# Keys' and values' block products move to a third PSUM bank, queries take turns with the other two, and the last sequence's output shares are cut by heads

## The chip, the cores and the metric

The kernel runs on one core of a Trainium2 chip. The metric is device time in microseconds (us) of one execution, lower is better. The core's engines are TensorE (PE; its weight loads are the row PEld), VectorE (DVE), ScalarE (ACT), GpSimd (POOL) and SyncE (SP, which issues the DMAs). They work side by side and wait for each other by semaphores.

## What is computed

The input is 16 sequences of 256 tokens with 256 features, float32. Two residual layers follow each other:

```python
x = x + attention(layernorm(x), wq, wk, wv, wo)
x = x + quantised_linear(layernorm(x), weight, bias)
```

The attention has 16 query heads and 4 key and value heads of 128 features each, four query heads to a group. A query sees the first 4 keys (the sink) and the last 32, its own among them. The linear layer rounds its input, row by row, and its weight, output row by output row, to whole numbers from -128 to 127, multiplies, scales back and adds the bias.

## The kernel before

**Units and slots.** A unit is (n, g, t): a sequence n (0 to 15), a group g (0 to 3) of four heads, and a half t of the 256 tokens. There are 128 units, in the order of the list `units` (line 693), in which two of the last sequence change places, so that it ends (15,2,0), (15,3,0), (15,2,1), (15,3,1). The main loop (line 769) goes through slots i = 0 to 129. In slot i TensorE computes the scores of unit i, turns the exponentials of unit i-1, and multiplies those by the values. Everything else is put into slots by hand: `chunks` (keys or values), `asked` (queries), `shares` (output projection), `early` and `small` (all the rest). `in_written_order` (line 21) then holds every engine to the order in which its instructions were written, so that an instruction that waits holds up all behind it on its engine.

**One slot.** `scores_and_turned` (line 475) interleaves four score products into the bank `pss` with four transposes into the bank `ptd`. ScalarE copies `ptd` to `ad`; VectorE scales and masks the scores (L497) and takes the maximum (L499); ScalarE takes four exponentials (L506); VectorE divides by the sums (L513 to L516, the function `normalised`). The next slot's transposes `ptd` need that result. `times_values` (line 518) writes `po`, in the pool `ps_m`, and ScalarE copies it to `oT` (L531).

**Products by seven.** From the second sequence on, queries, keys and values of a pair of heads are 256x256 products made of seven 128x128 block products instead of eight (`products`, line 251), from sums that GpSimd has made beforehand. A float32 product of 128x128 blocks is two matmul instructions, so a group has 14. `REGION` (line 225) gives each product its place: 2, 6, 1 and 7 fill the first bank of a pair, 4, 5 and 3 three quarters of the second. `combine` (line 264) then adds them up in five steps, L276 to L280: L276 and L277 read the first bank, L278 to L280 the second. For queries VectorE does it in the following slot, straight from PSUM (ScalarE first copies product 1, L291). For keys and values (a *chunk*) ScalarE copies both banks in the same slot, the small one first (`both_banks`, L297), and GpSimd combines from the copies.

A query group issues 1, 2, 6, 7 and then 4, 5, 3; a chunk issues 4, 5, 3 first (`SMALL_FIRST`). Query groups come in every slot; chunks in four slots out of eight: for sequence n in slots 8n-5 and 8n+1 (values), 8n-3 and 8n-1 (keys). Queries of the first sequence, and heads 14 and 15 of the last one, are plain products (L464).

**PSUM.** There are eight banks: one for `pss`, one for `ptd`, two for the output projection (`y0`, `y1`), two for queries, keys and values (`q0`, `q1`, pool `ps_q`), and two that take turns in the pool `ps_m`. The latter hold `po`, the transposed input `xt` (line 341, slot 8n-7 for sequence n), `ht` and `pa` of the linear layer (lines 620 and 627), and plain products. `ps_m` hands its two tiles out in turn: a request gets the one asked for the longer time ago, and its first matmul waits until that has been read.

**Output and linear layer.** `projected_fast` (line 561) projects a group's heads with the same seven products for sequences 1 to 14; `projected` (line 547) does plain products, four heads at a time, for the first and last sequence, in slot i+2 (i+3 for some). The linear layer is five steps, `ffn_steps` (line 590): stats, norm, quantise, turn, linear, one in each of five slots. The last sequence has a shorter form for each half of its tokens, `last_steps` (line 641), run in slots 127 to 128 for the first half and after the loop for the second.

Of the kernel before, what the change touches and what calls it, by code (L numbers as in the profile page):

```python
# [34 lines left out]
def kernel(  # L35
# [148 lines left out]
    def ffn_weight_steps():  # L184
        ws = p1.tile([P, NC], FP, name="ws")
        wq16 = p1.tile([P, NC, DM], BF, name="wq16")
        diag = p1.tile([P, NC, P], FP, name="diag")

        wr = p1.tile([P, NC], FP, name="wr")

        def scales():
            dve.tensor_reduce(ws, wf_sb, AX.X, ALU.max, apply_absolute_value=True)
            dve.tensor_scalar(ws, ws, 1e-8, 1.0 / 127.0, ALU.max, ALU.mult)
            dve.reciprocal(wr, ws)

# [12 lines left out]
        def turn():  # L208
            for c in range(NC):
                pt = ps_m.tile([P, NC, P], BF, tag="m", name=f"wt_{c}")  # L210
                for o in range(NC):
                    pe.transpose(pt[:, o, :], wq16[:, o, c * P : (c + 1) * P], ident16)
                act.copy(wqfT[:, c, :], pt.rearrange("p o n -> p (o n)"))
            pw = ps_m.tile([P, DM], FP, tag="m", name="pw")
            for c in range(NC):
                pe.matmul(pw[:, c * P : (c + 1) * P], ones, diag[:, c, :], start=True, stop=True)
            act.copy(wsc_bc, pw)

        return [scales, quantise, diagonals, narrow, turn]

# [1 line left out]

    REGION = {2: (0, 0), 6: (0, 1), 1: (0, 2), 7: (0, 3), 4: (1, 0), 5: (1, 1), 3: (1, 2)}

    def banks(pool_, tag, name):
        return [pool_.tile([P, NBLK, P], FP, tag=f"{tag}{k}", name=f"{name}_{k}") for k in range(2)]

    def region(p, i):  # L230
        return p[REGION[i][0]][:, REGION[i][1]]
# [27 lines left out]
            yield region(p, i), *pairs[i]  # L259


    SMALL_FIRST = (4, 5, 3, 1, 2, 6, 7)

    def combine(eng, p, p1, c11_u, v, c12, c21_c22):

# [156 lines left out]

    def keys(n, pair):

        p = banks(ps_q, "q", f"pk_{n}_{pair}")[::-1]
        for to, left, right in products(p, factors(n, wk_sb, wk_sums, pair), SMALL_FIRST):
            pe.matmul(to, left, right, start=True, stop=True)  # L427
        k = p1.tile([P, 2, 3, D], FP, tag="ktmp", name=f"ktmp_{n}_{pair}")
        kb = k[:, :, 0:2].rearrange("p e j (k i) -> p e (j k) i", i=QB)
        rest = lambda: keys_to(n, 2 * pair, kb)  # L430
        keys_late[rest] = 1 + pair
        return Products(p, f"k_{n}_{pair}", (k[:, 0, 0:3:2], k[:, 1, 2], k[:, 0, 1], k[:, 1, 0:2])), rest

    def values(n, pair):
        p = banks(ps_q, "q", f"pv_{n}_{pair}")[::-1]
        for to, left, right in products(p, factors(n, wv_sb, wv_sums, pair), SMALL_FIRST):
            pe.matmul(to, right, left, start=True, stop=True)  # L437
        v = p2.tile([P, 3, 2, D], FP, tag="vt", name=f"vt_{n}_{pair}")
        w = vw[n, pair] = p3.tile([NK, SB, 2 * D], FP, tag="vw", name=f"vw_{n}_{pair}")
        return Products(p, f"v_{n}_{pair}", (v[:, 0:3:2, 0], v[:, 2, 1], v[:, 1, 0], v[:, 0:2, 1])), (  # L440
            lambda: values_to(w, v.rearrange("p j e d -> p j (e d)"), range(NT))
        )

    def queries(n, h):

        g, hh = divmod(h, HG)
        if hh == 0:
            qt[n, g] = p2.tile([P, NT + 1, NBLK, HG, QB], FP, tag="qt", name=f"qt_{n}_{g}")
        q = qt[n, g]
        if fast_queries(n, h):  # L450
            p = banks(ps_q, "q", f"pq_{n}_{h}")
            for to, left, right in products(p, factors(n, wq_sb, wq_sums[:, g], h // 2)):
                pe.matmul(to, left, right, start=True, stop=True)  # L453
            return Products(
                p, f"q_{n}_{h}", (q[:, 0:3:2, :, hh], q[:, 2, :, hh + 1], q[:, 1, :, hh], q[:, 0:2, :, hh + 1])
            )
        if hh == 0:
            pq = ps_q.tile([P, NBLK, P], FP, tag="q0", name=f"pq_{n}_{h}")
            pq = pq.rearrange("p (e j) i -> p e (j i)", e=2)
        else:  # L460
            pq = ps_m.tile([P, 2, T], FP, tag="m", name=f"pq_{n}_{h}")
        for e in range(2):
            for c in range(NC):
                pe.matmul(  # L464
                    pq[:, e], wq_sb[:, c, (h + e) * D : (h + e + 1) * D], xnT[n][:, c, :],
                    start=(c == 0), stop=(c == NC - 1),
                )
        to = q[:, 0:NT, :, hh : hh + 2, :].rearrange("p t k h i -> p h (t k) i")
        return lambda: act.copy(to, pq.rearrange("p h (k i) -> p h k i", i=QB))
# [74 lines left out]
        t = [wo_sums[:, i, 2 * g : 2 * g + 2] for i in range(4)]  # L544
        right_sums(t, *(wo_half(g, p, half) for p in range(2) for half in range(2)))

    def projected(n, g, t):

        if (g, t) == (0, 0):
            pys[n] = banks(ps_y, "y", f"py_{n}")  # L550
        py, o = pys[n][t][:, 0:2].rearrange("p i d -> p (i d)"), oTs[n, g]
        last = n == B - 1
        if last and g == 0:
            pe.matmul(py, ident, xts[n][:, t, :], start=True, stop=False)
        for hh in range(HG):
            h = g * HG + hh
            pe.matmul(py, o[:, t, hh, :], wo_sb[:, h, :], start=(h == 0 and not last), stop=(h == H - 1))  # L557
        if g == G - 1 and not last:
# [2 lines left out]
    def projected_fast(n, g, part):  # L561

        if (g, part) == (0, 0):
            pys[n] = banks(ps_y, "y", f"py_{n}")
# [12 lines left out]
        if (g, part) == (G - 1, 1):  # L577
# [3 lines left out]
            def rest():  # L581
                sums.first()
                sums.combine(dve)
                xt = xts[n].rearrange("p t (i d) -> p (t i) d", d=D)
                (pool if n < B - 2 else dve).tensor_add(xt, xt, f[:, 0:4])

            return rest

# [52 lines left out]
    def last_steps(j):  # L641
# [2 lines left out]

        n, tag = B - 1, f"last_{j}"
        py = pys[n][j][:, 0:2].rearrange("p i d -> p (i d)")
        d, x2 = (p1.tile([P, NT, DM], FP, tag=k, name=f"{k}_{tag}")[:, 0] for k in ("h", "yo"))
        y = p1.tile([P, NT, DM], FP, tag="xn", name=f"y_{tag}")[:, 0]
        mv = p2.tile([P, nc.vector.BN_AGGR_DIM], FP, tag="mv2", name=f"mv_{tag}")
        top, by, xs = (p2.tile([P, 1], FP, tag=k, name=f"{k}_{tag}") for k in ("top", "by", "xs1"))  # L650
# [13 lines left out]
        def quantise():  # L664
            dve.tensor_scalar(top, top, mv[:, 1:2], 127e-12, ALU.mult, ALU.max)
            dve.reciprocal(by, top)
            dve.tensor_scalar(by, by, mv[:, 1:2], 127.0, ALU.mult, ALU.mult)
            dve.tensor_scalar(d, d, by, MAGIC, ALU.mult, ALU.add)
            dve.tensor_scalar(d, d, MAGIC + 127.0, MAGIC - 128.0, ALU.min, ALU.max)
            pool.tensor_scalar(xs, top, 1.0 / 127.0, None, ALU.mult)  # L670

        def turn():
            pt = ps_m.tile([P, NC, P], FP, tag="m", name=f"ht_{tag}")
            for c in range(NC):
                pe.transpose(pt[:, c], d[:, c * P : (c + 1) * P], ident)
            dve.tensor_scalar(hT, pt, MAGIC, None, ALU.subtract)

        def linear():
            pa = ps_m.tile([P, DM], FP, tag="m", name=f"pa_{tag}")
# [14 lines left out]
    units[-3], units[-2] = units[-2], units[-3]  # L694
    PER = G * NT

    chunks, early, asked, shares, small = {}, {}, {}, {}, {}

    def at(slot, f, what=small):
        what.setdefault(slot, []).append(f)  # L700

    for n in range(B):
        q = (-3, -2, -1, 0, 1, 2, 3, 4) if n < B - 1 else (-3, -2, -1, 0, 1, 2, 3, 3)
        if n == 0:
            q = (-1, -1, 0, 0, 1, 1, 2, 4)
            for slot, f in (
# [13 lines left out]
        at(max(first + 2, 2), lambda n=n: turned(n))  # L720
        at(max(first - 5, 0), lambda n=n: n > 1 and load_x(n))
    for i, (n, g, t) in enumerate(units):
        if not fast_output(n):
            late = n == 0 or i == (B - 1) * PER
            at(i + 3 if late else i + 2, lambda u=(n, g, t): projected(*u), shares)
        elif t == 1:
            for part in range(2):
                at(i + 2 + part, lambda u=(n, g, part): projected_fast(*u), shares)
# [3 lines left out]
        at((2, 3, 4, 6)[g], lambda g=g: weight_sums(wq_sb[:, :, g * HG * D : (g + 1) * HG * D], wq_sums[:, g]))  # L732
        at(7 + g, lambda g=g: output_weight_sums(g))
    at(0, other_loads)
    for slot, f in zip((3, 4, 7, 8, 10), ffn_weight_steps()):
        at(slot, f)
    steps = {}
    for n in range(B - 1):
        done = (n + 1) * PER + 2
        for k, slot in enumerate((1, 2, 3, 4, 5) if n < B - 2 else (0, 1, 2, 3, 4)):  # L740
            def step(n=n, k=k):
                if k == 0:
                    steps[n] = ffn_steps(n)
# [25 lines left out]
    for i in range(len(units) + 2):  # L769
# [3 lines left out]
        if waiting:  # L773
            waiting.first()
        shared = shares.pop(i, [])
        combined = [f() for f in shared]
        if u:
            sm = exponentials(*u, nmax)
        if waiting:
# [2 lines left out]
        rests = [f() for f in early.pop(i, []) if i]  # L782
        if not shared:
            rests += [queries(n, h) for n, h in asked.pop(i, []) if not fast_queries(n, h)]
        if i == len(units):
            tail[2]()
        values_out = times_values(*w) if w else None
        if chunk:
            chunk, chunk_rest = chunk()
            chunk.both_banks()  # L790
        if u:
            normalised(*u, sm)
        for f in rests:
            f()
        if w:
            values_out()
        for f in later.pop(i, []):
# [13 lines left out]
        for f in combined:  # L811
            if f:
                f()
        for f in small.pop(i, []):
            f()
        if i == len(units) - 1:
            tail = last_steps(0)
            for f in tail[:2]:
                f()
        if i == len(units):  # L820
            tail[3]()
    for f in last_steps(1):
        f()
    in_written_order(tc)
# [32 lines left out]
```

## Time and profile before

| what | value |
|---|---|
| median of 3 runs | 816.11 us (815.9 to 816.27) |
| the profiled execution | 816.0 us |
| its span, first to last instruction | 814.2 us |
| mean granted TensorE clock | 0.997 |
| instructions | 19607 |
| matmuls | 7082 |
| period of a sequence (eight slots) in the middle | about 49.3 us |
| HBM read and written | 9.83 MB and 4.19 MB |

In the profile, a row of a timeline gives the start in us, the busy time in us, the engine, the line, the operation, what is written and read, and the number of instructions; brackets tell for how long the engine had been idle and what ended that. The chain of waits goes back from the last instruction, at each step to what released it or to the instruction before it on its engine; its rows give start, length, engine, tile, line and count. L453 is line 453. The period above is the distance from the keys' first group at 393.10 us to that of the next sequence at 442.29 us, rounded.

### The profile page before, as it was taken

The numbers are of one execution on the slowest core, as the hardware profiler recorded it, in microseconds if no ns is written. First come the engines' busy times: TensorE is split into PE (matmuls) and PEld (weight loads), VectorE is DVE, ScalarE is ACT, GpSimd is POOL, SyncE is SP. The second block draws the span as 40 slices with busy tenths as digits, with TensorE's granted clock in tenths as the row PEclk, the third lists the DMA queues.
The fourth block names the chain that finished last, engine by engine and source line by source line (L and its number), as shares of the span: only waits on it lengthen the run. The fifth ranks groups of instructions, "written<-read, shape, count | busy, mean of one in ns | idle before, by whom it ended". The sixth has DMA issues, their size and how long they took to land.

```text
span 814.2 us, 19607 instructions
## 1 busy us (share of the span) xinstructions
PE 800.1 (98%) x7082; PEld 785.5 (96%) x7082; DVE 588.1 (72%) x1711; ACT 441.9 (54%) x1631; POOL 511.2 (63%) x809
## 2 busy tenths in 40 slices
PE   9999999999999999999999999999999999999995
PEld 7899999999999999999999999999999999999984
DVE  2567777787777877877777877877877777777665
ACT  3655555555556555555555555555555555555552
POOL 4667775676576675676666666665766766756422
PEclk9999999999999999999999999999999999999998
DMA  6510201011020110201102020110202102010100
GB/s 213 160 28 14 57 14 46 25 36 48 16 59 11 52 32 14 70 14 42 29 27 58 14 52 20 41 42 15 63 7 56 29 20 64 14 33 25 32 11 27
DMA packets 35633, 33.14 MB, mean 41 GB/s; under 512 B 5968, under 2 KB 34000, under 8 KB 35536
## 3 DMA queue, kind: packets, MB, share of 16 engines
q1 hardware_dynamic: 35536, 31.87, 14.2%
q8 instruction: 57, 0.93, 0.5%
q14 instruction: 40, 0.33, 0.1%
HBM read 9.83 MB, written 4.19 MB: 17 GB/s over the span
## 4 chain that ended last, share of the span: by engine, by line
PE 95%; DVE 2%; ACT 1%; issue 0%; DMA 0%; POOL 0%; DVEq 0%; ACTq 0%; POOLq 0%
PE pq L453 23%; PE py L573 22%; PE po L522 14%; PE pss L486 11%; PE ptd L491 7%; PE pk L427 6%; PE pv L437 6%; PE py L557 3%; PE pq L464 1%; PE xt L344 1%; PE pa L630 1%; ACT s L506 1%; PE pv L399 0%; PE ht L623 0%; DMA x<-in_x_dram 0%
## 5 line engine op out<-in xcount | busy, mean ns | idle before, releaser
L494 ACT COPY ad<-ptd 68x512 f32<-68x512 f32 x128 | 74.4, 581 | 214.7 <-PE ptd L491 214.7
L506 ACT ACTIVATE s<-s,nmax 128x68 f32<-128x68 f32 x512 | 173.6, 340 | 18.8 <-DVE nmax L499 12.4
L486 PE MATMUL pss<-kt,qt 128*128 128x68 f32 x1024 | 152.5, 251 | 0.0
L486 PEld LDWEIGHTS pss<-kt,qt 128*128 128x128 f32 x1024 | 147.5, 191 | 0.8 <-issue 0.5
L491 PE MATMUL ptd<-ident,s 128*68 128x128 f32 x512 | 139.1, 273 | 1.8 <-ACT oT L531 1.0
L522 PE MATMUL po<-ad,vw 68*128 68x128 f32 x1024 | 135.4, 275 | 0.0
L497 DVE SCALAR_TENSOR_TENSOR s<-pss,masks 128x272 f32<-128x272 f32 x128 | 56.3, 440 | 108.8 <-PE pss L486 106.4
L522 PEld LDWEIGHTS po<-ad,vw 68*128 68x128 f32 x1024 | 125.7, 192 | 1.0 <-ACT ad L494 0.3
L453 PE MATMUL pq<-xs,wq_sums 128*128 128x128 f32 x714 | 118.7, 275 | 0.0
L453 PEld LDWEIGHTS pq<-xs,wq_sums 128*128 128x128 f32 x714 | 98.8, 192 | 0.0
L506 ACT ACTIVATION_READ_ACCUMULATOR s<-s,nmax 128x1 f32 x512 | 95.6, 187 | 0.0
L531 ACT COPY oT<-po 128x512 f32<-128x512 f32 x128 | 75.3, 588 | 28.8 <-PE po L522 28.8
L491 PEld LDWEIGHTS ptd<-ident,s 128*68 128x68 f32 x512 | 84.5, 165 | 2.3 <-ACT oT L531 2.3
L573 PE MATMUL py<-wo_sums,os 128*128 128x128 f32 x672 | 84.2, 275 | 0.0
L276 POOL TENSOR_TENSOR ktmp<-b_k 128x256 f32<-128x256 f32 x30 | 21.9, 729 | 94.7 <-ACT b_k L297 94.7
L573 PEld LDWEIGHTS py<-wo_sums,os 128*128 128x128 f32 x672 | 79.4, 192 | 0.0
L240 POOL TENSOR_TENSOR os<-oT 128x256 f32<-128x256 f32 x56 | 46.2, 825 | 43.9 <-ACT oT L531 42.1
L276 POOL TENSOR_TENSOR vt<-b_v 128x256 f32<-128x256 f32 x30 | 21.8, 728 | 82.8 <-ACT b_v L297 82.8
L453 PE MATMUL pq<-xnT,wq_sb 128*128 128x128 f32 x476 | 72.7, 275 | 0.0
L453 PEld LDWEIGHTS pq<-xnT,wq_sb 128*128 128x128 f32 x476 | 62.7, 192 | 0.2 <-ACT b_v L297 0.2
L516 DVE TENSOR_TENSOR s<-s,sm 128x272 f32<-128x272 f32 x128 | 58.9, 460 | 4.4
L573 PE MATMUL py<-wo_sb,oT 128*128 128x128 f32 x448 | 59.2, 275 | 0.0
(182 smaller groups left out, 1845.4 us busy)
## 6 DMA issues: line engine op xcount, KB each, us to landing
vw<-vt SPq DMA_DIRECT2D x192, 64.0 KB, 2.0
vw<-vt SPq DMA_DIRECT2D x160, 32.0 KB, 2.4
x<-in_x_dram SPq DMA_DIRECT2D x16, 256.0 KB
out_dram<-y SPq DMA_DIRECT2D x15, 256.0 KB, 2.1
wq_sb<-in_wqT_dram SPq DMA_DIRECT2D x4, 512.0 KB, 9.4
wo_sb<-in_woT_dram SPq DMA_DIRECT2D x4, 512.0 KB, 5.7
wv_sb<-in_wvT_dram SPq DMA_DIRECT2D x1, 512.0 KB, 3.8
wk_sb<-in_wkT_dram SPq DMA_DIRECT2D x1, 512.0 KB, 5.1
```

The source lines that it names most:

```text
L427: pe.matmul(to, left, right, start=True, stop=True)
L437: pe.matmul(to, right, left, start=True, stop=True)
L453: pe.matmul(to, left, right, start=True, stop=True)
L486: pe.matmul(pss[:, k, :], qt[n, g][:, t, k].rearrange("p h i -> p (h i)"), kt[n, g][:, t * NBLK + k, :], start=True, stop=True,)
L491: pe.transpose(ptd[:, k * P : (k + 1) * P], sw[:, k, :], ident)
L494: act.copy(ad, ptd)
L497: dve.scalar_tensor_tensor(s, pss, SCALE, masks[:, t], ALU.mult, ALU.add)
L506: act.activation(s[:, k, :], s[:, k, :], AF.Exp, bias=nmax[:, k : k + 1], scale=1.0, accum_out=sm[:, k : k + 1],)
L516: dve.tensor_mul(s, s, sm.unsqueeze(2).to_broadcast([P, NBLK, NK]))
L522: pe.matmul(po[:, k].rearrange("p h i -> p (h i)"), vw[n, g // 2][:, t * NBLK + k, g % 2 * D : (g % 2 + 1) * D], ad[:, k * P : (k + 1) * P ...
L531: act.copy(o[:, t].rearrange("p h (k i) -> p k h i", i=QB), po)
L573: pe.matmul(region(py, i), left[:, e], right[:, e], start=(g == 0 and e == 0 and i in (1, 4)), stop=(g == G - 1 and e == 1 and i in (7, 3)),)
```

## The change

The change is in the places of PSUM tiles and in the order of work:

1. A chunk's first bank (products 1, 2, 6, 7) is now a tile of `ps_m`; its second bank (4, 5, 3) is `q0` or `q1`, whose turn it is, and the turn then passes. A query group takes the bank whose turn it is first and the other second.
2. The spreading of the weight's scales (`pw`) leaves step `turn` of the weights and becomes a step of its own, one slot later (11).
3. In a slot, the rests of the early plain products are written ahead of `normalised` instead of behind it.
4. Sequence 14's linear layer starts one slot later, as those of the others; its sum goes to GpSimd, as theirs do. Heads 14 and 15 of the last sequence are computed in slot 124, not 123.
5. The last sequence's output shares go to slots by pairs of heads, after the list `LAST`.
6. The last sequence's first half: statistics and quantising are written ahead of the slot's small work; its transposes (`turn`) come at the end of slot 128, its product (`linear`) in slot 129 between the two pairs of heads. For both halves the rounding, the transposes and the subtraction of MAGIC go by 128 features, the transposes into `ps_s` and `ps_t`; d and x2 lie in other tiles.

The core of the diff:

```diff
+        def spread_scales():
             pw = ps_m.tile([P, DM], FP, tag="m", name="pw")
             for c in range(NC):
                 pe.matmul(pw[:, c * P : (c + 1) * P], ones, diag[:, c, :], start=True, stop=True)
             act.copy(wsc_bc, pw)
-        return [scales, quantise, diagonals, narrow, turn]
+        return [scales, quantise, diagonals, narrow, turn, spread_scales]
...
+    turn_of = [0]
+
+    def q_bank(other, name):
+        return ps_q.tile([P, NBLK, P], FP, tag=f"q{turn_of[0] ^ other}", name=name)
+
+    def banks_of_chunk(name):
+        p = [ps_m.tile([P, NBLK, P], FP, tag="m", name=f"{name}_0"), q_bank(0, f"{name}_1")]
+        turn_of[0] ^= 1
+        return p
...
-        p = banks(ps_q, "q", f"pk_{n}_{pair}")[::-1]
+        p = banks_of_chunk(f"pk_{n}_{pair}")
...
-        p = banks(ps_q, "q", f"pv_{n}_{pair}")[::-1]
+        p = banks_of_chunk(f"pv_{n}_{pair}")
...
-            p = banks(ps_q, "q", f"pq_{n}_{h}")
+            p = [q_bank(k, f"pq_{n}_{h}_{k}") for k in range(2)]
...
-            pq = ps_q.tile([P, NBLK, P], FP, tag="q0", name=f"pq_{n}_{h}")
+            pq = q_bank(0, f"pq_{n}_{h}")
...
-        for hh in range(HG):
+        for hh in heads:
...
-                (pool if n < B - 2 else dve).tensor_add(xt, xt, f[:, 0:4])
+                pool.tensor_add(xt, xt, f[:, 0:4])
...
-        d, x2 = (p1.tile([P, NT, DM], FP, tag=k, name=f"{k}_{tag}")[:, 0] for k in ("h", "yo"))
+        d = p1.tile([P, 2, 3, D], FP, tag="ktmp", name=f"d_{tag}")[:, 0, 0:2].rearrange("p i d -> p (i d)")
+        x2 = p1.tile([P, 6, D], FP, tag="pc", name=f"x2_{tag}")[:, 0:2].rearrange("p i d -> p (i d)")
...
-            dve.tensor_scalar(d, d, by, MAGIC, ALU.mult, ALU.add)
-            dve.tensor_scalar(d, d, MAGIC + 127.0, MAGIC - 128.0, ALU.min, ALU.max)
             pool.tensor_scalar(xs, top, 1.0 / 127.0, None, ALU.mult)
+            for c in range(NC):
+                k = d[:, c * P : (c + 1) * P]
+                dve.tensor_scalar(k, k, by, MAGIC, ALU.mult, ALU.add)
+                dve.tensor_scalar(k, k, MAGIC + 127.0, MAGIC - 128.0, ALU.min, ALU.max)
...
-            pt = ps_m.tile([P, NC, P], FP, tag="m", name=f"ht_{tag}")
-            for c in range(NC):
-                pe.transpose(pt[:, c], d[:, c * P : (c + 1) * P], ident)
-            dve.tensor_scalar(hT, pt, MAGIC, None, ALU.subtract)
+            for c in range(NC):
+                pt = (ps_s, ps_t)[c].tile([P, P], FP, tag="st"[c], name=f"ht_{tag}_{c}")
+                pe.transpose(pt, d[:, c * P : (c + 1) * P], ident)
+                dve.tensor_scalar(hT[:, c], pt, MAGIC, None, ALU.subtract)
...
+    LAST = ((3, 3), (4, 5), (5, 5), (6, 6), (6, 7), (7, 7), (8, 8), (9, 9))
...
-        q = (-3, -2, -1, 0, 1, 2, 3, 4) if n < B - 1 else (-3, -2, -1, 0, 1, 2, 3, 3)
+        q = (-3, -2, -1, 0, 1, 2, 3, 4)
...
-        if not fast_output(n):
-            late = n == 0 or i == (B - 1) * PER
-            at(i + 3 if late else i + 2, lambda u=(n, g, t): projected(*u), shares)
+        if n == 0:
+            at(i + 3, lambda u=(n, g, t): projected(*u), shares)
+        elif n == B - 1:
+            for slot, heads in zip(LAST[i % PER], ((0, 1), (2, 3))):
+                at(slot + i - i % PER, lambda u=(n, g, t, heads): projected(*u), shares)
...
-    for slot, f in zip((3, 4, 7, 8, 10), ffn_weight_steps()):
+    for slot, f in zip((3, 4, 7, 8, 10, 11), ffn_weight_steps()):
...
-        for k, slot in enumerate((1, 2, 3, 4, 5) if n < B - 2 else (0, 1, 2, 3, 4)):
+        for k, slot in enumerate((1, 2, 3, 4, 5)):
...
-        combined = [f() for f in shared]
+        combined = []
+        for k, f in enumerate(shared):
+            combined.append(f())
+            if i > len(units) and k == 0:
+                tail[3]()
...
-        if i == len(units):
-            tail[2]()
         values_out = times_values(*w) if w else None
         if chunk:
             chunk, chunk_rest = chunk()
             chunk.both_banks()
+        for f in rests:
+            f()
         if u:
             normalised(*u, sm)
-        for f in rests:
-            f()
...
-        for f in small.pop(i, []):
-            f()
         if i == len(units) - 1:
             tail = last_steps(0)
             for f in tail[:2]:
                 f()
+        for f in small.pop(i, []):
+            f()
         if i == len(units):
-            tail[3]()
+            tail[2]()
```

More of the change, by code (lines that the diff above doesn't have):

```diff
@@ L217, in turn, with y_banks @@
             act.copy(wsc_bc, pw)
-        return [scales, quantise, diagonals, narrow, turn]
+        return [scales, quantise, diagonals, narrow, turn, spread_scales]
     REGION = {2: (0, 0), 6: (0, 1), 1: (0, 2), 7: (0, 3), 4: (1, 0), 5: (1, 1), 3: (1, 2)}
-    def banks(pool_, tag, name):
-        return [pool_.tile([P, NBLK, P], FP, tag=f"{tag}{k}", name=f"{name}_{k}") for k in range(2)]
+    def y_banks(name):
+        return [ps_y.tile([P, NBLK, P], FP, tag=f"y{k}", name=f"{name}_{k}") for k in range(2)]
     def region(p, i):
@@ L545, in output_weight_sums, with projected @@
         right_sums(t, *(wo_half(g, p, half) for p in range(2) for half in range(2)))
-    def projected(n, g, t):
-        if (g, t) == (0, 0):
-            pys[n] = banks(ps_y, "y", f"py_{n}")
+    def projected(n, g, t, heads=range(HG)):
+        if (g, t, heads[0]) == (0, 0, 0):
+            pys[n] = y_banks(f"py_{n}")
         py, o = pys[n][t][:, 0:2].rearrange("p i d -> p (i d)"), oTs[n, g]
         last = n == B - 1
-        if last and g == 0:
+        if last and g == heads[0] == 0:
             pe.matmul(py, ident, xts[n][:, t, :], start=True, stop=False)
-        for hh in range(HG):
+        for hh in heads:
             h = g * HG + hh
@@ L563, in projected_fast @@
         if (g, part) == (0, 0):
[L564 removed]
+            pys[n] = y_banks(f"py_{n}")
         py, o, s = pys[n], oTs[n, g], o_sums[n, g]
```

## The prediction, made before the result was known

> **What bounds the kernel.** I read the page first, then the chain of waits by time, then the timelines of single engines. TensorE is busy for 98% of the span and carries 95% of the chain that ended last:
> ```profile
> PE 800.1 (98%) x7082; PEld 785.5 (96%) x7082; DVE 588.1 (72%) x1711; ACT 441.9 (54%) x1631; POOL 511.2 (63%) x809
> ...
> PE   9999999999999999999999999999999999999995
> ...
> PE 95%; DVE 2%; ACT 1%; issue 0%; DMA 0%; POOL 0%; DVEq 0%; ACTq 0%; POOLq 0%
> ```
> But a busy share hides small stalls, since matmul rows overlap. The chain lists start, length and count, and there a float32 128x128 matmul takes 0.1117 us from start to start (8 in 0.89), so a group of 14 should take 1.56. A stretch of one sequence:
> ```profile
> 392.21 0.89 PE po L522 x8
> 393.10 0.70 PE pk L427 x6
> 393.86 1.13 PE pk L427 x8
> 394.99 1.61 PE pq L453 x14
> ...
> 400.41 1.56 PE pq L453 x14
> ...
> 417.99 1.58 PE pv L437 x14
> 419.57 1.61 PE pq L453 x14
> 421.18 0.44 PE xt L344 x4
> ```
> A query group alone takes 1.56; behind keys or values 1.61; this keys group takes 1.89 and stops after its sixth matmul. VectorE's timeline names the reason: the last step of the combination of the queries before it, which reads the second query bank:
> ```profile
> 393.43 0.29 DVE L280 TENSOR_TENSOR qt<-pq,qt 128x128 f32<-128x128 f32 x1
> ```
> It ends at 393.72; TensorE goes on at 393.86 with product 1, which goes into that bank. The query group's 0.05 comes at its product 4, which goes into the bank that ScalarE empties last:
> ```profile
> 395.03 0.58 ACT L297 COPY b_k<-pk 128x512 f32<-128x512 f32 x1 [0.67 <-PE pk L427]
> 395.51 0.59 ACT L531 COPY oT<-po 128x512 f32<-128x512 f32 x1
> ```
> The copy ends at 395.61, product 4 starts at 395.72: a release within some 0.2 us still costs a little. The end is another regime. There TensorE idles openly, each time for the softmax or the last tile's quantisation:
> ```profile
> 785.17 0.27 PE L491 MATMUL ptd<-ident,s 128*68 128x128 f32 x1 [0.66 <-DVE xr L611]
> ...
> 789.65 0.28 PE L491 MATMUL ptd<-ident,s 128*68 128x128 f32 x1 [0.28 <-ACT oT L531]
> ...
> 798.60 0.60 PE L491 MATMUL ptd<-ident,s 128*68 128x128 f32 x4 [0.73 <-ACT oT L531]
> ...
> 801.60 0.44 PE L675 MATMUL ht_last<-ident,h_last 128*128 128x128 f32 x2 [0.67 <-DVE h_last L669]
> ...
> 803.60 1.99 PE L557 MATMUL py<-wo_sb,oT 128*128 128x256 f32 x8 [0.46 <-ACT oT L531]
> 808.89 0.41 PE L675 MATMUL ht_last<-ident,h_last 128*128 128x128 f32 x2 [3.29 <-DVE h_last L669]
> ```
> All four `ptd` waits end 0.14 to 0.15 after L516, whatever releaser is named.
>
> [...] with two banks for queries, keys and values the 1.89 appears. [...] the query group starts 0.33 late. [...] 256 elements take 424 ns (L276), 128 take 291 (L277).
>
> **The banks.** Chunks (keys, values) come in slots 3, 5, 7 and 1 of each eight, a query group in every slot. Before, a chunk puts products 4, 5, 3 into q0 and 1, 2, 6, 7 into q1. After, the four go to the pool `ps_m`, the three to the q bank whose turn it is (that of the last query group's big products, freed after L277, as before). The query group behind it starts in the bank that L280 frees, 14 matmuls after the chunk's start instead of 6: at 394.66 in the stretch above, 0.94 after L280. Its product 4 goes to the small bank, copied at 394.36, needed at 395.55. Both waits have 0.8 us or more to spare. Summed over the start times of all groups, the excess over 0.112 us a step, behind the first product of a chunk, is 4.7 us in 30 keys groups, 1.1 in 30 values groups and 2.7 in the 59 query groups behind them: 8.5. Some 0.2 lies at first uses, so I take **8.3**; ends 6.5 and 8.8. The first product's own 0.03 in slot 5 (wait for L277) stays.
> What this adds: `ps_m` has two tiles and now serves po, the chunk, and in slots 1 and 7 a third one (`xt`, `pa`), which takes over po's and so waits for ScalarE's `oT` copy, queued behind both chunk copies. Above it ends at 420.68 in slot 1, `xt` starts at 421.18; TensorE comes 0.08 sooner, the copy 0.03: 0.39 left with 0.06 of signalling. In slot 7 the copy ends at 408.32, `pa` starts at 408.82: the same. Hidden, **0**; the DVE and ACT work of a slot is the same, and L516 ends some 2 us before the next `ptd` in full slots.
>
> **The start.** In slot 2 `xt` stands 0.62 us, behind the `kt` copies of the plain keys (L372, L373, end 31.81). With the rests ahead of L513, L370 and L371 (0.69 + 0.62) run from 28.8, the ACT copies end near 30.5, before `xt` at 31.25; L516 moves to 31.0, wanted at 31.9. **0.6** (0.3 to 0.65). In slot 10 `pw` stands 0.46 for the first `wqfT` copy; moved to slot 11 it waits for `oT`, like `xt`, with 0.4 to spare: **0.45** (0 to 0.46).
>
> **The end, slot by slot (120 to 129).** Units of work on TensorE: scores and transposes 1.12, po 0.89, fast queries 1.56, plain queries 1.73, a whole share 1.73, two heads 0.86, x into py 0.43. From the last score to the next `ptd`: L497 0.44, L499 0.44, exponentials 1.45, L513 to L516 0.85, 0.14 and gaps: 3.43. Slot 123: 1.12 + 0.43 + 1.73 + 0.89 + 1.56 = 5.74 instead of 9.63. Slot 124: 1.12 + 0.43 + 0.86 + 0.89 + 1.73 = 5.04. Here the change adds a wait: the plain queries (heads 14, 15) are now last in slot 124, and slot 125, by the swapped order, scores group 3, which needs them. The copy L469 ended 0.79 after TensorE was free (781.22 against 780.43), with 0.06 for the signal **0.85**; everything on TensorE queues behind it. Slot 125: 1.12 + 0.86 + 1.73 + 0.89 = 4.60; slot 126: 1.12 + 1.73 + 0.86 + 0.89 + 0.27 for `ht` = 4.87. In both the work behind the scores exceeds 3.43, so the three `ptd` waits before 795 go. With 1.12 in slot 127 that is 22.22 to its last score, before 24.28 (770.80 to 795.08): gain 2.06.
> From there: 0.86 + 1.73 + 0.89 + `pa` 0.44 = 3.92, then `ptd` without a wait (3.43), share 1.73, po from 6.09. Its turn (after po) is ready near 6.3, but VectorE does sequence 14's L635 (0.96) before the two subtractions of MAGIC: 8.4. The last share's first heads start after the `oT` copy, po start + 1.73 = 7.82, end 8.68; then the moved `linear`, the other heads to 9.76; L682 and L683 end at 10.23, so L655 starts at 10.26, before at 10.56: gain 0.3. The moved steps' other instructions lie beside this: sequence 14's sum on POOL (1.28 for 0.69 on VectorE) has slot 123 before its statistics; its output DMA is issued near 9 (L635, then 1.27 on POOL), on SP before both last tiles' and landing in 2 us, before the end. On POOL the tile's L657, L658, L662 and L670 now stand ahead of that sum (L636), and need nothing from it. `ktmp` and `pc`, where the last tile's d and x2 move, were last used in slots 121 and 123.
> Halves of the last tile: four instructions of 0.27 and 0.22 (L203 takes 0.268 at 128) for 0.35 + 0.29, +0.4; the transposes and subtraction of half one overlap it and only one matmul is left at the end, -0.5: gain **0.1**, between -0.2 and 0.3.
> The end gains 2.06 + 0.3 + 0.1 = **2.5** (0.8 to 3.6).
>
> **Sum.** 8.3 + 0.6 + 0.45 + 2.5 = 11.9. The profiled run took 816.0 (span 814.2, 1.8 around it), so 804.1; the median, 816.11, is 0.1 above it: **804.2**.
>
> **Rivals.** *Third tile waits* (slower): ScalarE's `oT` copy comes late, and `xt`, `pa` and `pw`, 29 in all, stand for it. For it: the copy is behind two others and its slack is only 0.39. Against: its position to the chunk's end is fixed by 0.58 + 0.59. It decides from 11.9 / 29 = 0.41 us of wait each, a copy 0.8 later; at 0.5 each, 14.5, it gives 818.7. *The wait moves*: the query group behind a chunk now starts in the bank freed last, and inherits the stall; only start and end gain, 3.6: 812.5. Against: 0.94 to spare. *The end gives nothing*: the new 0.85 wait, and VectorE busy with L635 and more instructions, eat it: 806.7. For: there, slack is some 0.3 us per slot.
>
> **Chances.** Forecast 0.80 (own range 802.4 to 806), end gives nothing 0.10, wait moves 0.05, third tile 0.03, change elsewhere without effect 0.02. The best ends of banks, start and end give 802.6, the worst 808.4; they won't all fall together, so 802.4 to 807. A measurement tells 0.2%, 1.6 us, from none: faster 0.95, same 0.02, slower 0.03.
>
> **What would show it.** In the chain all 14-groups at 1.56 to 1.60, none split; `xt` and `pa` without idle time before them; a new wait of 0.85 before `pss` in slot 125 with `qt` L469 as releaser, none before `ptd`; L655 of the second tile near 793.9. Wrong if 14-groups stay at 1.61 or 1.89, or if idle time stands before `xt` and `pa`.

## The result, and the profile after

The changed kernel takes **803.58 us** (median of 4 runs, 803.49 to 803.93), against 816.19 (815.9 to 816.33) for the kernel before in the same comparison: ratio 0.9847, 95% interval 0.983 to 0.9864, or 12.6 us less. The profiled execution took 803.63, its span 801.8 instead of 814.2, at a mean granted clock of 0.998 (before 0.997). The forecast was 804.2, with a range from 802.4 to 807.0.

In the page of the changed kernel the busy share of TensorE has risen by one point only, but the chain that ended last is now TensorE's for 98% of the span instead of 95%:

```profile
PE 791.8 (99%) x7082; PEld 780.4 (97%) x7082; DVE 588.9 (73%) x1716; ACT 442.2 (55%) x1631; POOL 514.1 (64%) x810
...
PE   9999999999999999999999999999999999999996
...
PE 98%; DVE 1%; DMA 0%; POOL 0%; issue 0%; ACT 0%; DVEq 0%; POOLq 0%
```

PE's busy time fell by 8.3 us with the same 7082 matmuls: rows of waiting matmuls overlap (a row of L466 lasts 275 ns, at 112 from start to start), so a stall inside a group had been counted as busy. Of the 0.33 us that the keys group at 393.10 lost in the kernel before, the chain shows only 0.06 as a gap between its two rows. The chain of the changed kernel by time, for the stretch shown of before (keys are now line 440, values 450, queries 466, `xt` 357, `pa` 644):

```profile
387.69 1.59 PE pk L440 x14
389.28 1.56 PE pq L466 x14
...
399.86 1.56 PE pk L440 x14
401.42 1.56 PE pq L466 x14
402.98 0.44 PE pa L644 x4
...
412.16 1.56 PE pv L450 x14
413.72 1.56 PE pq L466 x14
415.28 0.44 PE xt L357 x4
```

No keys group is split any more, the query groups behind chunks take 1.56 like those that stand alone, and `pa` and `xt` follow at once. Only the keys group of slot 5 keeps 0.03. In TensorE's timeline of the changed kernel, the end shows one new wait, and no idle time ahead of any `ptd` (L504, before L491):

```profile
772.59 0.44 PE L499 MATMUL pss<-kt,qt 128*128 128x68 f32 x2 [0.68 <-ACT qt L482]
...
777.48 0.27 PE L504 MATMUL ptd<-ident,s 128*68 128x128 f32 x1
...
782.38 0.27 PE L504 MATMUL ptd<-ident,s 128*68 128x128 f32 x1
...
787.26 0.60 PE L504 MATMUL ptd<-ident,s 128*68 128x128 f32 x4
...
791.22 1.13 PE L571 MATMUL py<-wo_sb,oT 128*128 128x256 f32 x4 [0.46 <-ACT oT L544]
...
796.56 0.79 PE L692 MATMUL ht_last<-ident,d_last 128*128 128x128 f32 x2 [3.13 <-DVE d_last L687]
```

The second half's statistics, in VectorE's timeline, come at 793.54 (before 805.64; forecast "near 793.9"):

```profile
793.54 0.42 DVE L670 BATCH_NORM_STATS2 st_last<-py 128x6 f32<-128x256 f32 x1
```

The two traces, laid side by side by the first score product of a slot, say where the 12.4 us of span went:

| stretch | before | after | gain | forecast |
|---|---|---|---|---|
| start to slot 0 | 15.91 | 15.71 | 0.20 | 0 |
| slot 0 to slot 123 | 754.89 | 745.25 | 9.64 | 9.35 |
| slot 123 to the end of slot 127's scores | 24.28 | 22.37 | 1.91 | 2.06 |
| from there to the second half's statistics | 10.56 | 10.21 | 0.35 | 0.3 |
| from there to the end of the span | 8.56 | 8.26 | 0.30 | 0.1 |

The 0.20 ahead of slot 0 is no effect of the change: it varies from run to run (15.66 to 15.91 in most kernels here, 17.74 in one). Nor is all of the last row, as is shown below: there the granted clock of the two executions differs.

### The profile page after: what moved, and what is told of

It reads as the page before. It is cut to its first block, busy times and chain, and to the rows that moved or that the text cites. A ratio compares the mean times of both kernels' runs of the same rounds, so it can differ in the third digit from the quotient of the medians.

```text
span 801.8 us, 19597 instructions
## 1 busy us (share of the span) xinstructions
PE 791.8 (99%) x7082; PEld 780.4 (97%) x7082; DVE 588.9 (73%) x1716; ACT 442.2 (55%) x1631; POOL 514.1 (64%) x810
## 4 chain that ended last, share of the span: by engine, by line
PE 98%; DVE 1%; DMA 0%; POOL 0%; issue 0%; ACT 0%; DVEq 0%; POOLq 0%
PE pq L466 23%; PE py L587 22%; PE po L535 14%; PE pss L499 11%; PE ptd L504 7%; PE pk L440 6%; PE pv L450 6%; PE py L571 3%; PE pq L477 2%; PE xt L357 1%; PE pa L644 1%; PE pk L403 0%; PE pv L412 0%; PE ht L637 0%; DMA x<-in_x_dram 0%
## 5 line engine op out<-in xcount | busy, mean ns | idle before, releaser
L504 PE MATMUL ptd<-ident,s 128*68 128x128 f32 x512 | 139.1, 273 | 0.0
L466 PE MATMUL pq<-xs,wq_sums 128*128 128x128 f32 x714 | 118.6, 275 | 0.0
L466 PEld LDWEIGHTS pq<-xs,wq_sums 128*128 128x128 f32 x714 | 98.8, 192 | 0.0
L504 PEld LDWEIGHTS ptd<-ident,s 128*68 128x68 f32 x512 | 84.7, 165 | 0.1
L466 PE MATMUL pq<-xnT,wq_sb 128*128 128x128 f32 x476 | 72.6, 275 | 0.0
L466 PEld LDWEIGHTS pq<-xnT,wq_sb 128*128 128x128 f32 x476 | 62.7, 192 | 0.0
L529 DVE TENSOR_TENSOR s<-s,sm 128x272 f32<-128x272 f32 x128 | 58.9, 460 | 4.4
```

What stands on the lines that cost most here:

```text
L504: pe.transpose(ptd[:, k * P : (k + 1) * P], sw[:, k, :], ident)
L529: dve.tensor_mul(s, s, sm.unsqueeze(2).to_broadcast([P, NBLK, NK]))
```

## The experiments

Each kernel starts from the kernel before (the first two) or from the changed one. The changed kernel and the experiments were measured in four comparisons, in which the median of the kernel before was 816.03 to 816.43. A difference below some 0.2 us between two medians is therefore not taken for an effect; where it matters, the traces are compared slot by slot.

**The banks alone.** The kernel before with the new places of the tiles and nothing else:

```diff
+    def q_bank(other, name):
+        return ps_q.tile([P, NBLK, P], FP, tag=f"q{turn_of[0] ^ other}", name=name)
+
+    def banks_of_chunk(name):
+        p = [ps_m.tile([P, NBLK, P], FP, tag="m", name=f"{name}_0"), q_bank(0, f"{name}_1")]
+        turn_of[0] ^= 1
+        return p
...
-        p = banks(ps_q, "q", f"pk_{n}_{pair}")[::-1]
+        p = banks_of_chunk(f"pk_{n}_{pair}")
```

> The kernel before with the change of banks alone: chunks' first bank in ps_m, query groups and chunks' second bank take turns. My theory (TensorE's small stalls at shared banks are the main gain): 8.4 us faster than before, about 807.7, every 14-group behind keys or values at 1.56 to 1.60. Rival (the wait only moves to the query group, or the end makes the gain): within 2 us of before, groups of 1.61 and 1.89 stay or new idle time stands before xt and pa.

Measured: 807.18 us (806.95 to 807.48), ratio 0.9891 (0.9875 to 0.9908), 8.85 less than the kernel before in this comparison (816.03). Slot 123 starts 8.74 earlier, of which 0.23 lies ahead of slot 0; 8.5 is left. The banks carry some 70% of the gain; the rival in which the wait moves to the query groups (812.5) is out.

**The start alone.** The kernel before with `rests` ahead of `normalised` and `spread_scales` as a step in slot 11:

```diff
+        for f in rests:
+            f()
         if u:
             normalised(*u, sm)
-        for f in rests:
-            f()
```

> The kernel before with only the order in slot 2 (rests ahead of the normalisation) and the spreading of the scales one slot later. My theory: the 0.62 us before xt in slot 2 and the 0.46 before pw go, 1.05 us faster than before, about 815.1. Rival (the normalisation, now later, is waited for): the 0.62 stands before ptd in slot 3 instead, gain 0.45 or less.

Measured: 814.7 (median of 20 runs, 814.34 to 816.83), ratio 0.9986 (0.9979 to 0.9992), 1.33 less. In the trace slot 123 starts 1.38 earlier, of which 0.23 lies ahead of slot 0; 1.15 is left, against 1.05. `xt` of slot 2 starts at 31.01 without idle time.

**No turn.** The changed kernel, where chunks and queries always take `q0` first:

```diff
-        turn_of[0] ^= 1
```

> The changed kernel without the taking of turns: chunks still have their first bank in ps_m, but their second bank is always q0, and query groups always start in q0. The query group then starts in the chunk's small bank, whose copy ends some 0.3 us before. My theory (the third bank brings the gain, the turn only adds distance): 0 to 0.5 us slower than the changed kernel. Rival (the turn is needed, a release that close costs 0.05 as before): 59 groups at 1.61, 2.7 us slower.

Measured: 803.93 (803.68 to 804.01), ratio 0.9851 (0.9836 to 0.9866), 0.35 more than the changed kernel. All groups stay at 1.56 to 1.60 but two in slot 41, a values group and the queries behind it, which lose 0.19 and 0.10. There ScalarE starts the chunk's small copy 0.28 later than in the other chunks, in the changed kernel too; without the turn the queries start in that bank and wait. The gain comes from the third bank; the turn covers one late copy, 0.29 us in the trace.

**One more copy ahead of `oT`.** My theory was that `xt` and `pa` wait for ScalarE's `oT` copy, with 0.39 us to spare. A copy of 0.62 us whose output nobody uses goes in front of it in slots 1 and 7:

```diff
             chunk.both_banks()
+            if i % PER in (1, 7):
+                spare = p1.tile([P, 4, P], FP, tag="spare", name=f"spare_{i}")
+                act.copy(spare, chunk.p[0])
```

> The changed kernel with one more ScalarE copy of 128x512 (its result is not used) between a chunk's copies and the oT copy, in the slots with a third ps_m tile (1 and 7 of eight). ScalarE starts such copies 0.48 us apart, so oT ends 0.48 later, and xt and pa have 0.39 to spare. My theory: they now stand 0.1 to 0.2 us each, 28 or so times, 2.5 to 5.6 us slower, with oT named before xt and pa. Rival (the distance is larger than I reckoned, the third tile is no risk): less than 1 us slower.

Measured: 803.68 (803.49 to 803.88), ratio 0.9849 (0.9834 to 0.9863): nothing. **The theory fell.** ScalarE's timeline of this kernel has `oT` late, as meant:

```profile
413.79 0.58 ACT L310 COPY b_v<-pv 128x512 f32<-128x512 f32 x1 [0.36 <-PE pv L450]
414.41 0.62 ACT L817 COPY spare<-b_v 128x512 f32<-128x512 f32 x1
414.94 0.58 ACT L544 COPY oT<-po 128x512 f32<-128x512 f32 x1
```

It ends at 415.52. But TensorE's timeline has `xt` start before that, without idle time:

```profile
415.16 0.60 PE L357 MATMUL xt<-ident,xn 128*128 128x128 f32 x4
```

So `xt` doesn't take over the tile of `po`. The other candidate is the chunk's tile, whose copy (L310, 413.79) is written before `oT`'s and ends at 414.37.

**Three copies ahead of the chunk's copy.** To test that, three copies whose output nobody uses stand between the chunk's small and its large copy, in slots 1 and 7 only:

```diff
             for k in (1, 0):
                 act.copy(copies[k], self.p[k][:, 0 : 4 - k])
+                for j in range(3 * k * third):
+                    spare = p1.tile([P, 4, P], FP, tag="spare", name=f"spare_{self.tag}_{j}")
+                    act.copy(spare.rearrange("p a b -> p (a b)"), bias2)
```

> The changed kernel with three more ScalarE copies of 128x512 (their results are not used) ahead of the copy of a chunk's big bank, in the slots with a third ps_m tile. One more copy behind that bank's, ahead of oT, had cost nothing, so xt and pa do not take over po's tile, as I had predicted; if they take over the chunk's, the tile whose last reader is written first, then the big bank's copy now ends some 0.3 to 0.4 us after xt could start: 28 waits, 8 to 11 us slower than the changed kernel. Rival (the third tile waits for neither): less than 1 us slower.

Measured: 828.87 (828.67 to 829.03), ratio 1.0157 (1.014 to 1.0174), 25.3 more than the changed kernel. The waits of TensorE in this kernel (total, times, longest) name the copy:

```profile
PE xt L360 <- ACT b_v L310: 6.6, 14, 0.5
PE pa L647 <- ACT b_k L310: 5.8, 14, 0.4
PE ptd L507 <- DVE s L532: 5.0, 13, 0.4
```

In this kernel `pa` of one slot 7 starts at 415.43, 0.05 after the chunk's large copy ends and 0.43 before `oT` ends. So the releaser of the third tile is shown; the size was not foreseen. Against the changed kernel a sequence loses 0.58 us at `pa` and 1.24 in the slot of `xt`: 1.82, 14 times over 25.5. Of the 1.24, `xt` itself costs 0.69 by the starts of the instructions, and a wait before `ptd` 0.54. (The first sequence has no such `ptd` wait, but a keys group in slot 13 loses 0.64.) The 0.58 follows from the changed kernel's rows: there the large copy ends at 402.05 and `pa` starts at 402.82, so 0.72 is spare after 0.05 of signalling; the three copies make the large one 1.31 later. So the 0.3 to 0.4 a wait that I expected was too small, and the term that I had left out is the third row, a `ptd` that waits for the softmax: some 7 of the 25.3 us. VectorE's timeline of this kernel has the same small instruction (L529, four elements a partition) in two slots:

```profile
412.12 0.15 DVE L529 TENSOR_TENSOR sm<-sm,floor 128x4 f32<-128x4 f32 x1
...
419.61 1.22 DVE L529 TENSOR_TENSOR sm<-sm,floor 128x4 f32<-128x4 f32 x1
```

And GpSimd's timeline has what ran beside the second:

```profile
419.55 1.27 POOL L653 TENSOR_TENSOR y<-y,x 128x512 f32<-128x512 f32 x1
```

L529 ends at 420.83, GpSimd's addition at 420.82. The late keys' copy had pushed GpSimd's combination and this addition back, until they met the softmax. The trace of the changed kernel has the same on a smaller scale. Of its 128 such instructions (L526) the 92 with no GpSimd instruction beside them take 0.15 to 0.16 us, and so do 14 beside GpSimd's L631, a TENSOR_SCALAR; 20 take 0.24 to 0.71, and each of these ends 0.02 us after a TENSOR_TENSOR of GpSimd that was running when it started. What makes the one wait for the other, the runs do not show.

**Chunks with the large bank first.** The prediction took a release within some 0.2 us for costly. Here the chunks issue 1, 2, 6, 7 first and ScalarE copies in that order; the query group's product 4 then follows the release of its bank by little (the values have the same edit as the keys shown here):

```diff
-            for k in (1, 0):
+            for k in (0, 1):
                 act.copy(copies[k], self.p[k][:, 0 : 4 - k])
...
-        for to, left, right in products(p, factors(n, wk_sb, wk_sums, pair), SMALL_FIRST):
+        for to, left, right in products(p, factors(n, wk_sb, wk_sums, pair)):
```

> The changed kernel with chunks issuing products 1, 2, 6, 7 first and ScalarE copying that bank first. The small bank is then copied last, and the query group behind wants it some 0.2 us after the copy's end. If a release within 0.2 us costs 0.05, as the trace of before suggests: 59 groups of 1.61, less 0.5 for the first products that no longer wait for L277, 1 to 2.4 us slower. Rival (only a release that comes too late costs): 0.5 us faster.

Measured: 803.3 (803.22 to 803.42), ratio 0.984 (0.9825 to 0.9854), 0.3 less than the changed kernel, and slot 123 starts 0.58 earlier; 0.26 of this is lost again in the last stretch, where the granted clock of the profiled execution is lower (see below). **My 0.2 us fell.** ScalarE's timeline of this kernel:

```profile
388.08 1.15 ACT L310 COPY b_k<-pk 128x512 f32<-128x512 f32 x2 [0.50 <-PE pk L440]
```

The small copy ends at 389.23. TensorE's timeline has product 4 (the third row of the group) 0.16 later:

```profile
388.95 0.61 PE L466 MATMUL pq<-xs,wq_sums 128*128 128x128 f32 x4
389.39 0.39 PE L466 MATMUL pq<-xs,wq_sb 128*128 128x128 f32 x2
```

It starts 0.44 after the row ahead, four steps of 0.11: no stall. Of all 59 such groups 58 have the copy's end 0.16 to 0.22 ahead of product 4, and none of them loses more than 0.02 us. One, in slot 115, loses 0.27: its small copy starts 0.28 later than the others and ends at 717.87, product 4 starts at 717.92. The kernel before lost 0.05 a group with a release 0.11 ahead, in 58 of 59. What is gained here is, for 0.4 us, the keys' first product, whose 0.03 goes in 14 groups, since the bank it starts in is now a tile of `ps_m`; another 0.35 lies in slots 7 and 9, and its cause stays open.

**The plain queries ahead of `po`.** Heads 14 and 15 stay in slot 124, but stand ahead of its `po`, so that the new wait of slot 125 has cover:

```diff
-        if not shared:
+        if not shared or i == len(units) - 4:
```

> The changed kernel with the plain queries of heads 14 and 15 ahead of po in slot 124 instead of behind it, so that their copy lies beside po. My theory: the wait of 0.9 us before pss in slot 125 goes, but slot 125 then comes sooner than VectorE, which still has the norm of sequence 14 to do, and a wait of 0.1 to 0.55 comes before ptd in slot 126; 0.3 to 0.8 us faster than the changed kernel. Rival (nothing else is late there): the whole 0.9 us.

Measured: 802.71 (802.61 to 802.94), ratio 0.9833 (0.9818 to 0.9847), 0.87 less than the changed kernel, about what the wait cost, as the rival had it. Slot 127 starts 0.91 earlier. The wait that my theory put in its place is small: TensorE's timeline of this kernel, slot 126, has `ptd` 0.25 behind the scores ahead of it, where 0.17 is the pace:

```profile
776.32 0.34 PE L499 MATMUL pss<-kt,qt 128*128 128x68 f32 x2
776.57 0.27 PE L504 MATMUL ptd<-ident,s 128*68 128x128 f32 x1
```

**Heads 14 and 15 back in slot 123**, as before the change:

```diff
-        q = (-3, -2, -1, 0, 1, 2, 3, 4)
+        q = (-3, -2, -1, 0, 1, 2, 3, 4) if n < B - 1 else (-3, -2, -1, 0, 1, 2, 3, 3)
```

> The changed kernel with heads 14 and 15 back in slot 123, as before. My theory: no wait before pss, but slot 124 has only 2.36 us of other work beside a softmax chain of 3.77 (with a combination of queries in it), so ptd waits 1.4 us in slot 125: 0.5 us slower than the changed kernel. Rival (the move of the heads was a loss): 0.9 us faster.

Measured: 804.69 (804.43 to 804.76), ratio 0.9855 (0.9839 to 0.9872), 1.1 more than the changed kernel. The wait before `pss` is gone, but two before `ptd` are back, in TensorE's timeline of this kernel:

```profile
773.13 0.28 PE L504 MATMUL ptd<-ident,s 128*68 128x128 f32 x1 [0.87 <-DVE s L529]
...
778.35 0.27 PE L504 MATMUL ptd<-ident,s 128*68 128x128 f32 x1 [0.43 <-DVE xr L625]
```

Without the 1.73 us of these queries slot 124 is too short to cover the softmax. The loss is twice the 0.5 that I expected: up to the last score the trace loses 0.91, with a second wait that was not foreseen, and 0.26 more in the last stretch, by the clock.

**The old slots for the output shares:**

```diff
-    LAST = ((3, 3), (4, 5), (5, 5), (6, 6), (6, 7), (7, 7), (8, 8), (9, 9))
+    LAST = ((3, 3), (3, 3), (4, 4), (5, 5), (6, 6), (7, 7), (8, 8), (9, 9))
```

> The changed kernel with the last sequence's output shares back in whole and in their old slots (two in 123, then one each). My theory (the shares by heads fill what TensorE stood before ptd): ptd waits 0.64, 0.4 and 0.37 us in slots 126 to 128 again, 1.2 to 1.4 us slower than the changed kernel, about 804.9. Rival (the end gained by the moved linear layer and the other order): within 0.3 us of it.

Measured: 805.3 (805.07 to 807.33), ratio 0.9874 (0.9859 to 0.9888), 1.7 more than the changed kernel. The profiled execution is the slowest of these runs; it started its first scores 2.0 us late. From slot 123 to the second half's statistics it loses 1.55 against the changed kernel. Three waits before `ptd`, idle time of 0.56, 0.27 and 0.29 us, account for it: by the starts of the instructions they cost 0.72, 0.44 and 0.46. So the new slots of the shares are worth most of what the end gains. The edit moves the shares of four units, and only two of those are cut by heads; what the cut alone is worth, no run tells.

**The last tile whole.** Rounding, transposes and subtraction of both halves of the last sequence as in the kernel before:

```diff
-            for c in range(NC):
-                k = d[:, c * P : (c + 1) * P]
-                dve.tensor_scalar(k, k, by, MAGIC, ALU.mult, ALU.add)
-                dve.tensor_scalar(k, k, MAGIC + 127.0, MAGIC - 128.0, ALU.min, ALU.max)
+            dve.tensor_scalar(d, d, by, MAGIC, ALU.mult, ALU.add)
+            dve.tensor_scalar(d, d, MAGIC + 127.0, MAGIC - 128.0, ALU.min, ALU.max)
```

> The changed kernel with the last tiles rounded, transposed and reduced by MAGIC whole, not by halves. My theory: from the second tile's statistics to the end 0.1 to 0.3 us longer, too little for the time itself to tell, to be read in the trace. Rival (four short instructions cost more than they hide): shorter than by halves.

Measured: 804.23 (803.73 to 804.29), ratio 0.9849 (0.9835 to 0.9864), 0.65 more than the changed kernel. From the second statistics to the start of the last scaling it takes 5.13 us, the changed kernel 4.57. Not all of this is the halves. The kernel above with the early plain queries has the halves too and takes 4.83; its windows of one microsecond (length; busy PE, PEld, DVE, ACT, POOL; granted clock; DMA) show why:

```profile
794.00:795.00 1.00, 0.00 (x0) 0.00 (x0) 0.82 (x4) 0.24 (x1) 0.91 (x2) 0.98 0.02 4
795.00:796.00 1.00, 0.36 (x1) 0.18 (x1) 0.90 (x5) 0.00 (x0) 0.24 (x2) 0.50 0.00 0
```

The granted clock has fallen to half as its last transposes begin (795.64). In the changed kernel's profiled execution it holds through the last product:

```profile
797.00:798.00 1.00, 0.81 (x3) 0.33 (x3) 0.51 (x2) 0.00 (x0) 0.00 (x0) 1.00 0.00 0
798.00:799.00 1.00, 0.01 (x1) 0.00 (x0) 0.86 (x2) 0.00 (x0) 0.00 (x0) 0.91 0.00 0
```

The whole tile also ran at 0.60 and 0.50 there, so the like comparison is 5.13 against 4.83: at half clock the halves bring 0.3, and the clock is another 0.26.

**TensorE kept busy at the end.** 27 transposes whose output nobody uses, ahead of the last tile's transposes:

```diff
     for k, f in enumerate(last_steps(1)):
+        if k == 2:
+            fill = ps_m.tile([P, P], FP, tag="m", name="fill")
+            for _ in range(27):
+                pe.transpose(fill, ident, ident)
         f()
```

> The changed kernel with 27 transposes of the identity into an unused tile ahead of the second last tile's transposes, where TensorE stands 3.1 us. In the changed kernel's profile the granted clock stays 1.0 until the last matmul, in runs with nearly the same end it fell to 0.5 before, and the last stage took 8.26 against 8.5 to 8.6 us. Theory (the clock falls because TensorE stands, and when it falls is chance): granted clock 1.0 up to the last matmul and a last stage of 8.2 to 8.3 us, 0 to 0.3 us faster than the changed kernel. Rival (the clock has another cause): clock 0.5 there and 8.5 to 8.6 us in spite of the filler.

Measured: 803.52 (803.5 to 803.56), ratio 0.9847 (0.9832 to 0.9861), the changed kernel's time. It takes the same 4.57 us: TensorE idles for 0.18 us instead of 3.13 ahead of L692, but the changed kernel's clock had not fallen by then anyway. What shrank is the spread of the four runs, 0.06 us instead of 0.44. That this is the clock, the record of all runs makes likely: each lists its mean granted clock, and the time goes with it. Of the 20 runs of the start alone, the ten with 0.998 took 814.34 to 814.77, the seven with 0.996 took 814.75 or more. No kernel without the filling transposes has a run above 0.998, and most of their runs are at 0.996 or 0.997; all eight runs of the two kernels with them have 0.998 to 1.0. So some 0.3 us of a difference between two medians here can be the clock at the end.

**What worked, together:** early plain queries, large bank first, and the filling transposes.

> The three that help together: plain queries ahead of po in slot 124, chunks' big bank first, the filler at the end. If the gains add up: 0.9 + 0.5 us of the changed kernel's 803.6 and the fast last stage of 8.2 to 8.3, about 802.0. Rival (they share a slack): 802.7 or more.

Measured: **802.23** (802.17 to 802.26), ratio 0.9831 (0.9816 to 0.9845): 1.35 less than the changed kernel, and the fastest of all. The clock is 1.00 through its last products, and the last stretch takes 4.57 again. Up to the last score the gains of the two other edits add up, 0.53 and 0.83 us.

## Why the prediction was right, step by step

The sum is close, and chance had no large part in it: of the 12.4 us of span some 0.2 ahead of slot 0 and some 0.2 by the clock at the end are no effects of the change, and the 12.0 left stand against the 11.8 of the last column.

**The banks: right, a little small.** The forecast was 8.3; alone they bring 8.5 between slots 0 and 123 (8.85 by the medians), and with all else about 8.5 of the 9.64. The excess over 0.112 us a step, summed over the groups, was 4.9 in keys, 1.1 in values and 2.5 in the queries behind them; after, it is 0.3, -0.1 and -0.3. So the "0.2 at first uses" that I took off 8.5 isn't there. What stays in the keys is the 0.03 at the first product, in 14 groups.

**"Takes over po's": wrong, and it didn't matter.** The step failed in its cause. The text ahead of the prediction says that `ps_m` gives the tile asked for the longer time ago; the runs show `xt` and `pa` taking over the chunk's tile, the one whose last reader is written first. They wait for the large chunk copy, with 0.72 us to spare in slot 7, not for `oT` with 0.39. "Hidden, 0" held, with nearly twice the margin. The slower rival had the wrong gate for the same reason: a late `oT` costs nothing, and what would have turned the result is a chunk copy late enough. Made 1.31 us late, it does, and costs more than the waits that I priced, since GpSimd's work moves along with it.

**The start: right.** Forecast 0.6 in slot 2 and 0.45 at `pw`; the trace has 0.68 and, from slot 10 to 12, 0.63, in which the chunk of slot 11 has a part. Alone: 1.15 against 1.05.

**The end: right in place and size.** All four `ptd` waits went, and one wait came where it was forecast: 0.84 against 0.85 by the starts of the instructions (772.59 where 771.75 was possible), and the first step behind it takes 0.10 longer. So it is 22.37 us instead of 22.22 up to the last score. From there the forecast had 10.26 to the second statistics, measured 10.21. The slack behind the scores is as thin as stated: taking 1.73 us out of one slot, or moving the shares back, brings waits of 0.3 to 0.9 at once and 1.1 to 1.7 in all. The rival "the end gives nothing" is refuted by the table: 2.26 up to the second statistics.

**The halves: the right sign; the size was measured together with the clock.** The term was 0.1; the table has 0.3. The four instructions took 0.29, 0.23, 0.28 and 0.23, near the 0.27 and 0.22 of the forecast, so the cost was right. But in the kernel before, the clock fell just ahead of the last two products; TensorE's timeline there and the window from 809.3 on:

```profile
809.82 0.61 PE L681 MATMUL pa_last<-wqfT,hT_last 128*128 128x256 bf16 x2 [0.52 <-DVE hT_last L676]
```

```profile
809.30:810.50 1.20, 0.61 (x2) 0.13 (x2) 0.43 (x1) 0.00 (x0) 0.00 (x0) 0.56 0.00 0
```

The same pair took 0.38 for the first half of the tokens, at full clock (802.77). So 0.23 of the 0.3 is the clock, and 0.08 is left for the halves at full clock: an estimate from these rows, near the forecast of 0.1. No run has the whole tile at full clock throughout in its trace.

**"A release within some 0.2 us still costs a little": too wide.** 0.11 cost 0.05; 0.16 cost nothing.

## What to carry to other kernels

A group of matmuls that stalls in its middle shows as a longer group, not as idle time: sum the starts against the pace of an undisturbed group (here 1.89 us against 1.56), and the sum is the price of a bank. Which buffer a rotating pool hands out must be read from who releases it in a trace, or tested by delaying one reader, before a slack is computed from it. A late copy is priced with all that its other readers do later, their collisions included. Before two kernels that end in a long wait are compared to some tenths of a microsecond, look at the granted clock at their ends (here 1.00 against 0.50, worth 0.26 us).

## What the runs showed of the hardware that I had not expected

- A VectorE instruction on four elements a partition took 1.22 us instead of 0.15 beside a GpSimd addition, and ended 0.01 us after it.
- At the end TensorE stands for 3.1 us, 3.3 or 3.4 with the tile whole. There the granted clock fell to 0.50 before the last transposes in the kernels with one more copy, early plain queries, plain queries back, the whole tile and the large bank first: the mean of their last 8.3 to 8.8 us is 0.63 to 0.65. In the changed kernel and the one without the turn, which issue the same work there as all of these but the whole tile, it fell after the last product: 0.82 and 0.81 over the last 8.3 us. It is worth 0.26 us.
- The moment of the fall differs from execution to execution. In the changed kernel's profiled one it is 798.83, 5.29 us after the second statistics start (793.54); with the early plain queries 794.96, 2.34 after them (792.62); in the kernel before 809.45, 3.81 after them (805.64). What sets it, the runs do not show, so the changed kernel may have kept its clock to the last product by chance.
- In the profiled executions with the filling transposes the clock was 1.00 through the last product, and fell 0.8 and 1.2 us behind it.
